# Two-layer recurrent and attention block: the first pair's transposed input rounded by halves of its rows, and the last tile order at the end

## The chip, the cores and the metric

The kernel runs on one NeuronCore of a Trainium2 chip. The metric is the time of one execution on the device, in microseconds (us). The engines are called TensorE (PE in the profile, with its weight loads as PEld), VectorE (DVE), ScalarE (ACT), GpSimd (POOL) and SyncE (SP, which issues the transfers here).

## The reference

The input `x` has shape (4, 512, 256): four batches of 512 tokens. Two layers follow each other, and each has the same outer form:

```
xn = layernorm(x)
s  = attention_or_recurrence(xn)          # layer 0: recurrence, layer 1: causal attention
up_gate = xn @ W1.T ; up_lin = xn @ W3.T  # (tokens, 1024)
hidden  = fwht(silu(up_gate) * up_lin)    # Walsh-Hadamard transform
g  = silu(hidden @ W2.T)
x  = x + s * g
```

The recurrence starts from a zero state and takes one step, so it is a linear map of `xn` followed by an RMS norm, plus `xn`. The change touches the start of layer 0 (its layer norm, the transposition of `xn` and the first products with W1 and W3) and the end of layer 1 (the last products with W2, the Silu, and the final sum).

## The kernel before, in words

**Number format.** Every float32 operand of a product is split into a high part, rounded to the PE's reduced format by a ScalarE copy (CAST in the profile), and a low part, which is the difference taken by VectorE. A product is then three matmuls: high by high, low by high, high by low.

**Tiles.** A batch has four token tiles of 128 tokens. Activations are kept transposed (features on partitions) for the products with W1 and W3. `xT` of batch 0 is the tile `xt` in the profile, with two row halves `k` of 128 features each and 512 token columns. The hidden dimension of 1024 is worked in eight chunks `c` of 128, each with a gate half and a linear half (`f_0gu` in the profile, one bank of the accumulator memory each). Weights W1 and W3 come in four pieces `w13(q)`, q = 0 to 3, each for two chunks.

**The start.** `norm_first` (lines 379 to 428) does batch 0. VectorE takes the statistics of token tiles 0 and 1, then of 2 and 3, and writes `xn` one token tile at a time (line 404). In the meantime TensorE runs eleven products of zeros (`warm`, line 932), then the transposes of the first pair of token tiles, two more zero products, and the transposes of the second pair. A pair's four transposes (two token tiles by two row halves) fill one tile `xt0_0tp` of 128 by 512 float32, which is 2 KiB per partition. ScalarE copies it out as the high part (line 419), and VectorE subtracts for the low part (line 421). The order within each engine is written out by hand with `after(...)`, which puts an instruction behind another in its engine's order.

`split_w13` (line 122) splits a piece of W1 and W3; piece 0 is split in two halves, and the call `next(normed)` between them puts the second half of it behind the transposes.

**The first products.** In `ffn` (line 465) chunk 0 of batch 0 is worked in two halves of the tokens (`parts=2`), so that it can begin with the first pair of token tiles. For each half there are twelve products of 256 columns in three groups of four: high weights by high `xT`, low weights by high `xT`, high weights by low `xT` (line 517). Within a group the gate half takes both row halves `k`, then the linear half. Silu (line 526) and the product with the linear half (line 527) follow each chunk, and VectorE's queue then also holds the preparation of W2 (`w2b`, lines 155 and 156).

**The order elsewhere.** Outside the places with `after`, a scheduler orders each engine's instructions at build time from its own estimate of times. In layer 1 the TensorE order is fixed by hand (`line["fixed"]`).

**The end.** `ffn_s` for the last batch ends with a list of down products (lines 681 to 685): a unit is (q, c, t), three matmuls of 256 columns for token tile `t`. When a tile is complete, `gate_tile` (line 1055) does its Silu on ScalarE (line 1058), the product with `s` and the sum with `x` on VectorE (lines 1059 and 1060), and issues the store from SyncE (line 1061).

Of the kernel before, what the change touches and what calls it, by code (L numbers as in the profile page):

```python
# [35 lines left out]
def kernel(ctx: ExitStack, tc: tile.TileContext, a: dict, out: bass.AP):  # L36
    nc = tc.nc
# [21 lines left out]
    def split(src, hi, lo, engine=nc.vector):  # L59

        h = nc.scalar.copy(hi, src)  # L61
        return h, engine.tensor_tensor(lo, src, hi.bitcast(F32), ALU.subtract)  # L62
# [59 lines left out]
    def split_w13(layer, q, raw):  # L122
        both = wp.tile([P, 2, 2, S], F32R, tag="w13", name=f"w13_{layer}_{q}", bufs=4)
        hi, lo = both[:, 0], both[:, 1]
        if (layer, q) != (0, 0):
            split(raw, hi, lo)
            return hi, lo
        halves = [slice(c * D, (c + 1) * D) for c in range(2)]
        split(*(z[:, :, halves[0]] for z in (raw, hi, lo)))
        next(normed)  # L130
        with after(first["norm"][0]), after(first["norm"][1]):
            hi_, lo_ = split(*(z[:, :, halves[1]] for z in (raw, hi, lo)))
        first["w13"] = hi_, lo_
        return hi, lo
# [85 lines left out]
    def sl(i):  # L220
        return slice(i * P, (i + 1) * P)
# [157 lines left out]
    def norm_first():  # L379

        xn = act.tile([P, NT, D], F32, tag="xn", name="xn0_0", bufs=3)
        hi, lo = xTs[0, 0] = xt_pair("xt0_0")
        xns[0, 0] = xn
        x = xs[0]
        ins, pairs = None, []
        for i in range(2):
            st = act.tile([P, NT, 6], F32, tag="stats", name=f"ln0_0st{i}", bufs=4)
            mv = act.tile([P, NT, 2], F32, tag="mv", name=f"ln0_0mv{i}", bufs=4)
            r = small(f"ln0_0r{i}")
            with after(ins):  # L390
                for t in (2 * i, 2 * i + 1):
                    nc.vector.bn_stats(st[:, t, :], x[:, t, :])
                for t in (2 * i, 2 * i + 1):
                    nc.vector.bn_aggr(mv[:, t, :], st[:, t, :])
                rs = r[:, 2 * i : 2 * i + 2]
                ins = nc.vector.tensor_scalar(
                    rs, mv[:, 2 * i : 2 * i + 2, 1], LN_EPS, None, ALU.add
                )
            nc.gpsimd.tensor_tensor(rs, rs, mhalf[:, :2], ALU.pow)
            pairs.append((mv, r))  # L400
        for i, (mv, r) in enumerate(pairs):
            for t in (2 * i, 2 * i + 1):
                with after(ins):
                    ins = nc.vector.tensor_scalar(
                        xn[:, t, :], x[:, t, :], mv[:, t, 0:1], r[:, t : t + 1], ALU.subtract, ALU.mult
                    )
        yield

        hi_ = lo_ = None
        ins = zero_products(11)  # L410
        for i in range(2):
            ts_ = slice(2 * i * P, 2 * (i + 1) * P)
            o = psum(f"xt0_0tp{i}", [P, 2, 2 * P])
            with after(ins):
                for t in (2 * i, 2 * i + 1):
                    for k in range(2):
                        ins = transpose(o[:, k, sl(t - 2 * i)], xn[:, t, sl(k)], ident)
            with after(hi_):
                hi_ = nc.scalar.copy(hi[:, :, ts_], o)
            with after(lo_):  # L420
                lo_ = nc.vector.tensor_tensor(
                    lo[:, :, ts_], o, hi[:, :, ts_].bitcast(F32), ALU.subtract
                )
            if i == 0:
                with after(ins):
                    ins = zero_products(2)
        first["norm"] = hi_, lo_
        yield
# [33 lines left out]
    def after(ins):  # L462
        return tc.issue_after(ins.ins) if ins else nullcontext()

    def ffn(name, xT, w13, w2, slot, defer=1, spare=(), parts=1, behind=False, tail=()):

        w2h, w2l = w2  # L470
        dn, outs, firsts = [], [], {}

        def down(c, hh, hl, tiles=range(NT)):
            if not dn:
                dn.extend(psum(f"{name}dn{i}", [P, 2, D], tag="dn", bufs=2) for i in range(2))
                outs.extend(dn[t // 2][:, t % 2, :] for t in range(NT))
            for t in tiles:
                o = outs[t]
                for n, (l, r) in enumerate(((hh, w2h), (hh, w2l), (hl, w2h))):
                    first = c == 0 and n == 0  # L480
                    stop = c == NH - 1 and n == 2

                    def one(start):
                        return matmul(
                            o, l[:, sl(t)], r[:, c, :], start=start, stop=stop, skip_group_check=True
                        )

                    if first and t % 2 == 1:  # L490
                        with tc.issue_after(firsts[t // 2].ins):
                            ins = one(False)
                    elif first:
                        ins = firsts[t // 2] = one(True)
                    else:
                        ins = one(False)
            return ins

        queue, gates, late = [], [], []
        for c in range(NH):  # L500
            with after(gates[-2] if behind and c >= 2 else None):
                wh, wl = w13(c // 2)
            gu = []
            for j in range(2):

                o = psum(f"{name}gu{c}_{j}", [P, S], **(DN[0] if behind and c == 1 else GU))
                cols = slice((c % 2) * D + j * P, (c % 2) * D + (j + 1) * P)
                gu.append((o, cols))
            for half in range(parts if c == 0 else 1):
                n = S // (parts if c == 0 else 1)  # L510
                ts_ = slice(half * n, (half + 1) * n)
                if parts == 1 or c:
                    for o, cols in gu:
                        last_up = mm3(o[:, ts_], k_pairs((wh, wl), cols, xT, ts_))
                    continue

                for n, (w, x) in enumerate(((wh, xT[0]), (wl, xT[0]), (wh, xT[1]))):
                    for o, cols in gu:
                        for k in range(2):
                            last_up = matmul(  # L520
                                o[:, ts_], w[:, k, cols], x[:, k, ts_],
                                start=n + k == 0, stop=n + k == 3,
                            )
            gu = [o for o, _ in gu]
            h = hid(f"{name}h{c}")
            first["silu"] = nc.scalar.activation(h, gu[0], AF.Silu)
            gates.append(nc.vector.tensor_tensor(h, h, gu[1], ALU.mult))  # L527
            first["gate"] = gates[-1]
            if c < len(spare):
                hh, hl = spare[c]  # L530
            else:
                hh = hid(f"{name}hh{c}", F32R)
                hl = hid(f"{name}hl{c}", F32R)
            if c < len(spare):
                nc.scalar.copy(hh, h)
                late.append((hl, h, hh))
            else:
                split(h, hh, hl)
            for _ in range(2 if c >= NH - 2 else 0):
                if late:  # L540
                    lo_, h_, hi_ = late.pop(0)
                    with after(gates[-1]):
                        nc.vector.tensor_tensor(lo_, h_, hi_.bitcast(F32), ALU.subtract)
            queue.append((c, hh, hl))
            ups = last_up if behind else None
            with after(gates[-1] if behind else None), after(ups):
                slot(2 * c)
            if len(queue) > defer:
                down(*queue.pop(0))
            with after(gates[-1] if behind else None), after(ups):  # L550
                slot(2 * c + 1)
        line["fixed"] = bool(tail)
        line["last"] = last_up
        for what in tail:
            what()
        for q in queue:
            down(*q)
        return dn

    def ffn_s(name, b, pairs, w2, beside, before, last=None):  # L560
# [119 lines left out]
            return behind, dns  # L680
        for q, c, t in (
            (2, 0, 2), (2, 1, 2), (2, 0, 3), (2, 1, 3), (3, 0, 0), (3, 1, 0), (3, 0, 1), (3, 1, 1),
            (3, 0, 2), (3, 0, 3), (3, 1, 2), (3, 1, 3),
        ):
            down(q, c, hidden[q], (t,))
            if (q, c) == (3, 1):
                last(t, outs[t])
# [258 lines left out]
    first = {"table": None}  # L946
# [245 lines left out]
```

## Time and profile before

| | |
|---|---|
| median of 3 runs | 359.23 us (359.09 to 359.24) |
| the profiled execution's own time | 359.27 us |
| its span, first to last instruction | 357.5 us |
| TensorE busy (matmul, weight load) | 351.5 us, 327.4 us |
| VectorE, ScalarE, GpSimd busy | 287.1, 197.6, 20.8 us |
| mean share of the transfer engines | 41.0% on the main queue |

The span begins with the first instruction and ends with the last; the time of the execution has 1.8 us around it. Rows of the timeline give the start and the length of an instruction, or of several alike in a row (`x4`), in us from the start of the span, and in brackets the idle time of that engine just before and what ended it. Matmuls are pipelined, so a row of one matmul is longer than the step from one to the next. Tiles are named `out<-in`, without their buffer numbers.

### The profile page before, as it was taken

Reading aid. Unit: us, or ns where it says so; the run is one execution under the profiler, and the core shown is the slowest. Engines: PE = TensorE matmul, PEld = TensorE weight load, DVE = VectorE, ACT = ScalarE, POOL = GpSimd, SP = SyncE. Lnnn points to the kernel's source line nnn. Section 1 sums busy time; section 2 is a strip of 40 time slices with the busy share of each in tenths; the row PEclk is TensorE's granted clock in tenths of the full one; section 3 lists DMA queues with packets and bytes.
Section 4 is the critical chain, followed back from the end, with each engine's and each line's share of the span. In section 5 each row is a group of like instructions: output and inputs, shape, how many; then the busy total and the mean of one; then the engine's idle time right before and its main releaser. Section 6 shows DMA issues by size and latency. Waiting matters only on the chain.

```text
span 357.5 us, 6272 instructions
## 1 busy us (share of the span) xinstructions
PE 351.5 (98%) x2477; PEld 327.4 (92%) x2477; DVE 287.1 (80%) x597; ACT 197.6 (55%) x373; POOL 20.8 (6%) x22
## 2 busy tenths in 40 slices
PE   8999999999999999999999999999999999999995
PEld 6878998888988898888999999999999999999995
DVE  6899648998579938898887957989679897568645
ACT  3666156256373424674367655576555676556443
POOL 2000110300020210100110001100011000000000
PEclk9999999999999999999999999999999999999999
DMA  7935000301044416656357145562554745345401
GB/s 222 357 95 202 2 1 2 92 25 61 0 151 160 163 27 219 256 177 198 129 208 254 27 191 207 205 224 105 205 193 150 230 169 205 142 150 192 194 2 59
DMA packets 16284, 52.25 MB, mean 146 GB/s; under 512 B 1632, under 2 KB 7936, under 8 KB 16256
## 3 DMA queue, kind: packets, MB, share of 16 engines
q1 hardware_dynamic: 15968, 51.60, 41.0%
q8 instruction: 19, 0.31, 0.4%
q10 hardware_dynamic: 288, 0.26, 0.2%
q14 instruction: 9, 0.07, 0.1%
HBM read 42.40 MB, written 9.45 MB: 145 GB/s over the span
## 4 chain that ended last, share of the span: by engine, by line
PE 98%; DVE 1%; ACT 0%; issue 0%; DVEq 0%
PE f_1dn L70 6%; PE f_2dn L70 6%; PE f_1gu L70 6%; PE f_0dn L70 6%; PE f_0gu L70 6%; PE f_2gu L70 6%; PE f_3gu L70 6%; PE f_3dn L70 6%; PE sc L70 4%; PE pv L70 4%; PE o L70 3%; PE v L70 3%; PE tq L70 3%; PE warm L70 2%; PE w2ps L70 1%; PE pt L70 1%
## 5 line engine op out<-in xcount | busy, mean ns | idle before, releaser
L70 PE MATMUL f_1gu<-xt,w 128*128 128x512 f32 x96 | 24.9, 396 | 0.3 <-ACT xt L61 0.3
L70 PE MATMUL f_3gu<-xt,w 128*128 128x512 f32 x96 | 25.0, 396 | 0.0
L70 PE MATMUL f_2gu<-xt,w 128*128 128x512 f32 x96 | 24.8, 395 | 0.0
L70 PE MATMUL f_0gu<-xt,w 128*128 128x512 f32 (+1 forms) x108 | 24.4, 379 | 0.0
L70 PEld LDWEIGHTS f_0gu<-xt,w 128*128 128x128 f32 x108 | 18.5, 188 | 4.5 <-issue 1.0
L70 PEld LDWEIGHTS f_1gu<-xt,w 128*128 128x128 f32 x96 | 17.0, 188 | 3.6 <-ACT xt L61 0.5
L70 PEld LDWEIGHTS f_2gu<-xt,w 128*128 128x128 f32 x96 | 17.0, 188 | 3.0
L70 PEld LDWEIGHTS f_3gu<-xt,w 128*128 128x128 f32 x96 | 17.0, 188 | 2.9
L61 ACT CAST f_2hh<-f_2h 128x512 fp32r<-128x512 f32 x16 | 10.0, 622 | 15.3 <-DVE f_2h L527 12.2
L70 PE MATMUL f_3dn<-w2l,f_3hh 128*128 128x256 f32 x64 | 17.7, 281 | 0.0
L70 PE MATMUL f_1dn<-w2l,f_1hh 128*128 128x256 f32 x64 | 17.7, 281 | 0.0
L70 PE MATMUL f_3dn<-w2h,f_3hh 128*128 128x256 f32 x64 | 17.7, 281 | 0.0
L70 PE MATMUL f_2dn<-w2h,f_2hh 128*128 128x256 f32 x64 | 17.7, 282 | 0.0
L70 PE MATMUL f_1dn<-w2h,f_1hh 128*128 128x256 f32 x64 | 17.6, 280 | 0.0
L70 PE MATMUL f_2dn<-w2l,f_2hh 128*128 128x256 f32 x64 | 17.6, 280 | 0.0
L70 PE MATMUL f_3dn<-w2h,f_3hl 128*128 128x256 f32 x64 | 17.0, 281 | 0.0
L70 PE MATMUL f_1dn<-w2h,f_1hl 128*128 128x256 f32 x64 | 17.0, 281 | 0.0
L70 PE MATMUL f_2dn<-w2h,f_2hl 128*128 128x256 f32 x64 | 16.7, 281 | 0.0
L61 ACT CAST f_3hh<-f_3h 128x512 fp32r<-128x512 f32 (+1 forms) x17 | 10.0, 594 | 10.2 <-DVE f_3h L527 6.0
L61 ACT CAST f_1hh<-f_1h 128x512 fp32r<-128x512 f32 x16 | 9.9, 622 | 9.7 <-DVE f_1h L527 6.6
L62 DVE TENSOR_TENSOR f_2hl<-f_2h,f_2hh 128x512 fp32r<-128x512 f32 x16 | 11.0, 686 | 4.5 <-ACT f_2hh L61 4.5
L62 DVE TENSOR_TENSOR f_3hl<-f_3h,f_3hh 128x512 fp32r<-128x512 f32 (+1 forms) x17 | 11.1, 655 | 3.7 <-ACT f_3hh L61 3.6
(487 smaller groups left out, 1149.0 us busy)
## 6 DMA issues: line engine op xcount, KB each, us to landing
sw<-s SPq DMA_DIRECT2D x32, 896.0 KB, 5.3
s<-sp SPq DMA_DIRECT2D x8, 512.0 KB, 4.6
s<-sp SPq DMA_DIRECT2D x8, 384.0 KB, 2.8
w2raw<-in_w SPq DMA_DIRECT2D x4, 512.0 KB, 5.4
sraw<-in_w SPq DMA_DIRECT2D x4, 512.0 KB, 3.3
mrb<-there SPq DMA_DIRECT2D x4, 512.0 KB, 3.7
w13raw<-in_w SPq DMA_DIRECT2D x3, 512.0 KB, 6.8
x<-in_x SPq DMA_DIRECT2D x3, 512.0 KB, 3.6
```

What stands on the lines that cost most here:

```text
L61: h = nc.scalar.copy(hi, src)
L62: return h, engine.tensor_tensor(lo, src, hi.bitcast(F32), ALU.subtract)
L70: ins = call(*args, **kwargs)
```

## The change

There are four edits.

1. In `norm_first` the transposes of a pair run with the row half `k` outside and the token tile inside. For the first pair ScalarE rounds each row half by an instruction of its own, placed after that half's two transposes; for the second pair it rounds the whole as before.
2. In `ffn` the first chunk's products run with `k` outside and gate or linear half inside.
3. In `split_w13` the splits of pieces 2 and 3 are put behind the Silu of chunk 0 and of chunk 1.
4. In the list at the end, unit (3, 1, 2) goes ahead of unit (3, 0, 3).

```diff
     def split_w13(layer, q, raw):
         both = wp.tile([P, 2, 2, S], F32R, tag="w13", name=f"w13_{layer}_{q}", bufs=4)
         hi, lo = both[:, 0], both[:, 1]
-        if (layer, q) != (0, 0):
-            split(raw, hi, lo)
+        if q:
+            with after(first["silus"][q - 2] if q > 1 else None):
+                split(raw, hi, lo)
             return hi, lo
...
             o = psum(f"xt0_0tp{i}", [P, 2, 2 * P])
-            with after(ins):
-                for t in (2 * i, 2 * i + 1):
-                    for k in range(2):
+            for k in range(2):
+                with after(ins):
+                    for t in (2 * i, 2 * i + 1):
                         ins = transpose(o[:, k, sl(t - 2 * i)], xn[:, t, sl(k)], ident)
-            with after(hi_):
-                hi_ = nc.scalar.copy(hi[:, :, ts_], o)
+                if i == 0:
+                    with after(hi_):
+                        hi_ = nc.scalar.copy(hi[:, k, ts_], o[:, k, :])
+            if i:
+                with after(hi_):
+                    hi_ = nc.scalar.copy(hi[:, :, ts_], o)
             with after(lo_):
...
                 for n, (w, x) in enumerate(((wh, xT[0]), (wl, xT[0]), (wh, xT[1]))):
-                    for o, cols in gu:
-                        for k in range(2):
+                    for k in range(2):
+                        for o, cols in gu:
                             last_up = matmul(
...
             first["silu"] = nc.scalar.activation(h, gu[0], AF.Silu)
+            first.setdefault("silus", []).append(first["silu"])
...
             (2, 0, 2), (2, 1, 2), (2, 0, 3), (2, 1, 3), (3, 0, 0), (3, 1, 0), (3, 0, 1), (3, 1, 1),
-            (3, 0, 2), (3, 0, 3), (3, 1, 2), (3, 1, 3),
+            (3, 0, 2), (3, 1, 2), (3, 0, 3), (3, 1, 3),
```

## The prediction

> **What bounds the kernel now.** I read the page's busy times and its chain first, then the waits of TensorE and of its weight loads over the whole span, then the timeline of the two places that the change touches: the first ten microseconds and the last five.
>
> ```profile
> PE 351.5 (98%) x2477; PEld 327.4 (92%) x2477; DVE 287.1 (80%) x597; ACT 197.6 (55%) x373; POOL 20.8 (6%) x22
> ...
> PE 98%; DVE 1%; ACT 0%; issue 0%; DVEq 0%
> ```
>
> ```profile
> PE warm L70 <- DVE zr L929: 1.4, 1, 1.4
> PE f_1gu L70 <- ACT xt L61: 0.3, 1, 0.3
> ```
>
> TensorE is busy 98% of the span, and the chain is TensorE nearly throughout. Its real waits are the start (1.4 us) and one of 0.3 us at 51.6 us, which itself hangs on transposes that TensorE has just made. So a delay of TensorE near the start has nothing behind it that could swallow it: it goes to the end whole. What matters is when the first gate product starts. The timeline of 5 to 10.3 us, with narrow windows for single weight loads:
>
> ```profile
> 6.35 0.53 PEld L70 LDWEIGHTS xt_0tp<-ident,xn 128*128 128x128 f32 x4 [0.56 <-DVE xn L404]
> 6.67 0.15 PEld L70 LDWEIGHTS xt_0tp<-ident,xn 128*128 128x128 f32 x1
> 6.85 0.30 PEld L70 LDWEIGHTS warm<-zr 128*128 128x128 f32 x2
> 7.16 0.59 ACT L419 CAST xt<-xt_0tp 128x512 fp32r<-128x512 f32 x1 [0.56 <-PE xt_0tp L70]
> 7.36 0.53 PEld L70 LDWEIGHTS xt_0tp<-ident,xn 128*128 128x128 f32 x4 [0.20 <-DVE xn L404]
> 7.42 0.70 PE L70 MATMUL xt_0tp<-ident,xn 128*128 128x128 f32 x4
> 7.68 0.14 PEld L70 LDWEIGHTS xt_0tp<-ident,xn 128*128 128x128 f32 x1
> 7.85 2.62 PEld L70 LDWEIGHTS f_0gu<-xt,w 128*128 128x128 f32 x21
> 8.14 1.32 DVE L421 TENSOR_TENSOR xt<-xt_0tp,xt 128x512 fp32r<-128x512 f32 x2
> 8.88 0.19 PEld L70 LDWEIGHTS f_0gu<-xt,w 128*128 128x128 f32 x1
> ```
>
> The reader is to see that the first product's weight load (7.85) follows the second pair's last transpose at the usual step. That pair waits for VectorE's xn (loads at 7.36 and 7.68). ScalarE's rounding of the first pair is over at 7.16 + 0.59 = 7.75, before it is needed. **So what the first part of the change makes shorter is not what the first product waits for.**
>
> **The change part by part.** *1. The first pair by halves of its rows.* Before, four transposes fill one 2 KiB bank, and one ScalarE instruction rounds all of it while TensorE goes on in other banks. After, TensorE makes two transposes (row half k=0 of both token tiles), ScalarE rounds them, and TensorE then writes the k=1 transposes into the same bank. In the built program's order the third transpose now carries a wait for ScalarE, and that is the first of the two half roundings. It had none on ScalarE. Queued behind it on TensorE, in order, are the fourth transpose, two zero products, the second pair's transposes and every product of the kernel.
>
> The trace of before has no case of TensorE writing a bank that ScalarE is reading, so this wait is bounded from both sides. [...] By the row above alone (7.16, TensorE and ScalarE side by side in different banks) it would be nothing. [...]
>
> The working, from two rows: one of the view of the tile `xt_0tp`, for half a bank on ScalarE (minimum, median and longest in ns), and one of the timeline at 51.6 us:
>
> ```profile
> L756 ACT COPY b<-xt_0tp x1: 385/385/385, 145.0 to 145.0; 128x256 f32<-128x256 f32 x1
> ```
>
> ```profile
> 51.60 0.19 PEld L70 LDWEIGHTS f_1gu<-xt,w 128*128 128x128 f32 x1 [0.53 <-ACT xt L61]
> ```
>
> - The second transpose now has to wait for xn tile 1, as the third did: load at 6.67 as before. The four end at 7.12 (6.35 + 0.77 in the timeline), in steps of 0.11, so this one ends at 7.01.
> - ScalarE starts 0.04 after a transpose ends (7.12 to 7.16): 7.05. Half a bank takes 0.385: done at 7.43.
> - From ScalarE's end to TensorE's load: 0.05 (the cast before 51.60 runs from 50.97 for 0.58). The third transpose loads at 7.48 where it stood at 6.67: **+0.81**.
> - Slack behind it: the first transpose of the second pair starts at 7.42, just as the second zero product frees the array (7.19 + 0.23): none. Its third one is loaded at 7.68 for xn and not at about 7.58, as the step of 0.11 would have it: 0.10, which falls away. **-0.10**, so the first gate product comes 0.71 later.
> - Before, the ninth product waits for the low half of xT (load at 8.88, the one before it at 8.67, 0.21 instead of 0.12). After, the second half rounding ends at 7.93 + 0.04 + 0.385 = 8.36 and VectorE's subtraction at about 9.07, while TensorE needs it at 9.57. That stall goes: **-0.08**.
> - Next in line: the second pair's rounding ends near 9.45 and is needed at 9.97; the second half of the first weights is rounded by 9.97 and needed at 10.9; its low part ends near 10.75 and is needed at 12.65. All covered.
>
> *2. Products with k outside.* The same 16 products with the same loads: 0. But the gate bank is now finished by the second to last product, so the first Silu (11.76 before) comes one step, 0.12, later relative to TensorE, and with it the VectorE queue behind it. The tightest user is the low part of the second weights: VectorE ends it at 14.19 + 1.22 = 15.41, and its first load stands at 15.52. The cover is 0.06 after the 0.05 of the semaphore. But a load may come some 0.1 later before the product waits, since 512 columns take 0.23 and a load is followed by its product after 0.12. Between 0 and +0.06; I take **+0.02**.
>
> *3. Weights 2 and 3 not before the Silu of chunk 0 and 1.* In the built order only the rounding of weights 3 moves, ahead of one rounding of a hidden chunk on ScalarE. Their users come microseconds later (weights 3 from 25 us on; ScalarE idles there). Weights 2 wait for their transfer at 13.35, after the later Silu's end (about 13.1). No VectorE, GpSimd or SP instruction and no transfer changes its place. **0**.
>
> *4. The end.* Tile 2's last three products go ahead of tile 3's first group. Tile 2's Silu starts 0.35 earlier (352.56 for 352.92), but VectorE is busy with tile 1 until 353.33, and its order stays: product 2, product 3, sum 2, sum 3. Product 3 waits for tile 3's Silu, which waits for TensorE's last product, and that has not moved.
>
> ```profile
> 352.92 0.74 ACT L1058 ACTIVATE gl<-f_3dn 128x256 f32<-128x256 f32 x2 [0.68 <-PE f_3dn L70]
> ...
> 353.33 0.78 DVE L1059 TENSOR_TENSOR gl<-gl,xn 128x256 f32<-128x256 f32 x2
> ...
> 354.03 0.76 DVE L1060 TENSOR_TENSOR x<-x,gl 128x256 f32<-128x256 f32 x2
> ```
>
> So both sums, and the stores behind them on SP's queue, stand where they stood: **0**, at most -0.1 if the two Silus or two products crowd each other less than I read.
>
> **Sum:** 0.81 - 0.10 - 0.08 + 0.02 = +0.65 us. The profiled execution took 359.27 (span 357.5 and 1.8 around it) and the median is 359.23, so the sum moves over unchanged: 359.9. The lower end of the known costs is about +0.45 (a quicker restart of TensorE, 0.1 at the end). The upper is about +0.9: at 51.60 the restarted products stand 0.34 apart instead of 0.23, 0.1 more, and the tight cover of part 2 and some queue that I called covered may give the rest.
>
> **The rivals.**
> *A. The halves overlap as written: the third transpose doesn't lose by the wait.* It loads by about 6.78, so that the 0.10 of slack still hides it. Then part 1 costs nothing; it also gains nothing, for the first product is held by xn tile 3 and the stall at 8.88 by VectorE's queue (its weight subtraction runs from 7.54 to 8.23). 359.2, not slower. For it: the addresses are disjoint. Against it: the wait in the built order[...]. The point that decides is whether the third load is later than 6.78.
> *B. The clock.* TensorE starts slow: 11 zero products take 5.06 us, 0.43 apart, against 0.23 later. The new idle stretch of about 0.55 us comes just after it has become fast. [...] For it: the stretch falls in the first microsecond at the fast rate. Against it: [...]the idle stretch of 0.33 us at 51.6 slowed nothing after it.
> *C. Faster.* The end gives more than I read (sum 2 before product 3 would bring both stores forward, up to 0.4) and A holds as well: 358.8 to 359.1. The built order speaks against both.
>
> **How the numbers follow.** The main case (+0.65, 359.6 to 360.2) gets 0.86, A 0.06, B 0.05, C 0.03. About what a measurement of this kernel can tell from no change is 0.2%, 0.72 us, and my sum lies just under it. The terms left open (restart, tight cover, later queues) mostly point upward, so I put a little more than half of the main case above the line: 0.47 above, 0.39 below. Slower: 0.47 + 0.05 = 0.52. Within: 0.39 + 0.06 and part of C, 0.46. Faster: 0.02. The range from 359.4 to 360.4 takes in the bounds of the main case and leaves out most of A, B and C.
>
> **What would show it.** In the changed profile: ScalarE's rounding of the first pair as two rows of about 0.38; an idle stretch of about 0.6 on the weight loads, ended by ScalarE, with the third transpose's load near 7.48; the first gate load near 8.56; no gap where 8.88 stood; TensorE's last product about 0.65 later and everything after it unchanged. Wrong if the third transpose loads near 6.7 (A), if products of 256 columns stand 0.2 apart after 8.6 (B), or if the time from TensorE's last product to the end is shorter by more than 0.1 (C).

## The result: a loss of 0.62 us, from a wait before the third transpose

| | before | after |
|---|---|---|
| median of 17 runs each, on one chip | 359.19 us | 359.81 us |
| ratio, 95% interval | | 1.0021 (1.0013 to 1.003) |
| the profiled execution's own time | 359.27 us | 359.67 us |
| its span | 357.5 us | 357.9 us |

The change makes the kernel slower by 0.62 us. The page shows the same bound as before, TensorE, and the line of its chain reads word for word as it did before.

```profile
PE 351.4 (98%) x2477; PEld 327.4 (91%) x2477; DVE 287.0 (80%) x597; ACT 197.8 (55%) x374; POOL 20.8 (6%) x22
```

ScalarE has one instruction more (374), the second half rounding. What is new stands in the waits of TensorE over the whole span of the changed kernel (us in total, times, longest):

```profile
PE warm L70 <- DVE zr L935: 1.5, 1, 1.5
PE xt_0tp L70 <- ACT xt L421: 0.5, 1, 0.5
PE f_1gu L70 <- ACT xt L61: 0.3, 1, 0.3
```

The middle line did not exist before: the transposes (`xt_0tp`) wait once for ScalarE's copy out of their own tile. The timeline of the changed kernel from 5 to 10.9 us shows where:

```profile
5.73 0.73 DVE L405 TENSOR_SCALAR xn<-x,ln_0mv,ln_0r 128x256 f32<-128x256 f32 x2
...
6.51 0.14 PEld L70 LDWEIGHTS xt_0tp<-ident,xn 128*128 128x128 f32 x1 [0.18 <-DVE xn L405]
...
6.88 0.37 ACT L421 CAST xt<-xt_0tp 128x256 fp32r<-128x256 f32 x1 [0.25 <-PE xt_0tp L70]
...
7.31 0.20 PEld L70 LDWEIGHTS xt_0tp<-ident,xn 128*128 128x128 f32 x2 [0.65 <-ACT xt L421]
...
7.79 0.37 ACT L421 CAST xt<-xt_0tp 128x256 fp32r<-128x256 f32 x1 [0.53 <-PE xt_0tp L70]
7.83 0.59 PEld L70 LDWEIGHTS xt_0tp<-ident,xn 128*128 128x128 f32 x4
...
8.39 2.64 PEld L70 LDWEIGHTS f_0gu<-xt,w 128*128 128x128 f32 x22
```

Read it as a relay. The second transpose is loaded at 6.51. ScalarE rounds the first half from 6.88 to 7.25. The third transpose is loaded at 7.31, after the first of the two roundings and not beside it. Everything that TensorE still has to do stands behind it in order: the fourth transpose, two zero products, the second pair's transposes (7.83). So the first gate product is loaded at 8.39.

In this profiled execution VectorE happened to begin `xn` at 5.73 and not at 5.89 as in the trace of before, so the two traces are compared from there.

```profile
5.89 0.73 DVE L404 TENSOR_SCALAR xn<-x,ln_0mv,ln_0r 128x256 f32<-128x256 f32 x2
```

The first gate load comes 8.39 - 5.73 = 2.66 after `xn`, against 7.85 - 5.89 = 1.96 before: +0.70.

The last rows of TensorE, ScalarE and VectorE, from the timeline of the changed kernel from 352.2 us on:

```profile
352.96 0.38 ACT L1064 ACTIVATE gl<-f_3dn 128x256 f32<-128x256 f32 x1 [0.33 <-PE f_3dn L70]
...
353.01 0.75 DVE L1066 TENSOR_TENSOR x<-x,gl 128x256 f32<-128x256 f32 x2
...
353.36 0.28 PE L70 MATMUL f_3dn<-w2h,f_3hl 128*128 128x256 f32 x1
...
353.69 0.83 DVE L1065 TENSOR_TENSOR gl<-gl,xn 128x256 f32<-128x256 f32 x2
354.43 0.75 DVE L1066 TENSOR_TENSOR x<-x,gl 128x256 f32<-128x256 f32 x2
```

Tile 2's Silu (352.96) now runs before TensorE's last product ends, and is over at 353.34. But VectorE takes it up at 353.69 only, when it is nearly through with the sums of tiles 0 and 1 (the row at 353.01, which ends at 353.76). The two sums end at 355.18, which is 1.54 after the last product's end (353.64). Before they ended at 354.79, 1.55 after the end of the last product at 353.24 (its row is below). The end is unchanged to within 0.01.

A useful single number for all kernels below is the time from the first row of `xn` to the start of TensorE's last product, which leaves out when the input landed and what follows at the end. The row of before is (one product, 0.28 long; the product ahead of it starts at 352.84, 0.12 earlier)

```profile
352.96 0.28 PE L70 MATMUL f_3dn<-w2h,f_3hl 128*128 128x256 f32 x1
```

Before the time is 352.96 - 5.89 = 347.07, and after 353.36 - 5.73 = 347.63: +0.56 in these two executions, beside +0.62 in the medians.

### The profile page after: what moved, and what is told of

It reads as the page before. It is cut to its first block, busy times and chain, and to the rows that moved or that the text cites. A ratio compares the mean times of both kernels' runs of the same rounds, so it can differ in the third digit from the quotient of the medians.

```text
span 357.9 us, 6273 instructions
## 1 busy us (share of the span) xinstructions
PE 351.4 (98%) x2477; PEld 327.4 (91%) x2477; DVE 287.0 (80%) x597; ACT 197.8 (55%) x374; POOL 20.8 (6%) x22
## 4 chain that ended last, share of the span: by engine, by line
PE 98%; DVE 1%; ACT 0%; issue 0%; DVEq 0%
PE f_1dn L70 6%; PE f_2dn L70 6%; PE f_1gu L70 6%; PE f_0dn L70 6%; PE f_0gu L70 6%; PE f_2gu L70 6%; PE f_3gu L70 6%; PE f_3dn L70 6%; PE sc L70 4%; PE pv L70 4%; PE o L70 3%; PE v L70 3%; PE tq L70 3%; PE warm L70 1%; PE w2ps L70 1%; PE pt L70 1%
## 5 line engine op out<-in xcount | busy, mean ns | idle before, releaser
L61 ACT CAST f_2hh<-f_2h 128x512 fp32r<-128x512 f32 x16 | 9.9, 622 | 15.6 <-DVE f_2h L533 12.5
L62 DVE TENSOR_TENSOR f_2hl<-f_2h,f_2hh 128x512 fp32r<-128x512 f32 x16 | 10.9, 683 | 4.5 <-ACT f_2hh L61 4.5
```

## The experiments

The theory: the half rounding and the third transpose use one bank of the accumulator memory (a bank is here one buffer of the kernel's `psum` pool, 128 by 512 float32), the wait between them is the whole loss, and the other three edits are worth nothing. The rivals: the loss lies in another edit (the product order, the held weights, the end), or the halving itself costs, with or without the shared bank. Each kernel was timed beside the kernel before, whose medians were 359.22 (E1 to E4) and 359.23 (E5 to E8).

| kernel | median | ratio to before (95%) | first `xn` row to first gate load | to last product |
|---|---|---|---|---|
| before (profile as shown) | 359.19 to 359.23 | 1 | 1.96 | 347.07 |
| changed | 359.81 | 1.0021 (1.0013 to 1.003) | 2.66 | +0.56 |
| E1 all but edit 1 | 359.27 | 1.0002 (0.9994 to 1.0011) | 1.95 | -0.01 |
| E2 edits 1 and 3 | 359.79 | 1.002 (1.0013 to 1.0028) | 2.66 | +0.58 |
| E3 halves in two banks | 359.18 | 0.9998 (0.9989 to 1.0006) | 2.07 | -0.03 |
| E4 both pairs, in line | 360.47 | 1.0035 (1.0022 to 1.0049) | 3.39 | +1.32 |
| E5 both pairs | 359.82 | 1.0016 (1.0009 to 1.0022) | 2.42 | +0.59 |
| E6 no zero products | 359.44 | 1.0009 (1.0 to 1.0018) | 2.29 | +0.34 |
| E7 edit 1 alone | 361.69 | 1.0068 (1.0056 to 1.0081) | 2.65 | +3.05 |
| E8 the end on GpSimd | 360.16 | 1.0026 (1.0016 to 1.0035) | see there | see there |

### E1: all but the rounding

The changed kernel with edit 1 undone:

```diff
-            for k in range(2):
-                with after(ins):
-                    for t in (2 * i, 2 * i + 1):
+            with after(ins):
+                for t in (2 * i, 2 * i + 1):
+                    for k in range(2):
                         ins = transpose(o[:, k, sl(t - 2 * i)], xn[:, t, sl(k)], ident)
-                if i == 0:
-                    with after(hi_):
-                        hi_ = nc.scalar.copy(hi[:, k, ts_], o[:, k, :])
-            if i:
-                with after(hi_):
-                    hi_ = nc.scalar.copy(hi[:, :, ts_], o)
+            with after(hi_):
+                hi_ = nc.scalar.copy(hi[:, :, ts_], o)
```

> The changed kernel with the transposes and the rounding of the first pair as before; the other three edits (products with k outside, weights 2 and 3 behind the Silus, the order at the end) stay. If the bank wait is the whole cost: 359.2, no change from before (within 0.1), the stall ahead of the ninth product back, the first gate load at its old place 0.17 after the last transpose's load. If the k order of the products or the moved weights cost something: 359.5 or more. If the end alone gains: 359.1 or less, with the time from TensorE's last product to the end 0.1 shorter.

Measured 359.27, which can't be told from before. The first gate load is back at 1.95 after `xn`. The product order, the held weights and the end together are worth nothing measurable, so the loss needs edit 1.

### E2: the rounding and the weights alone

The changed kernel with edits 2 and 4 undone:

```diff
-                    for k in range(2):
-                        for o, cols in gu:
+                    for o, cols in gu:
+                        for k in range(2):
...
-            (3, 0, 2), (3, 1, 2), (3, 0, 3), (3, 1, 3),
+            (3, 0, 2), (3, 0, 3), (3, 1, 2), (3, 1, 3),
```

> The kernel before with the rounding by halves and the weights behind the Silus, without the k order of the products and without the new order at the end. If the bank wait is the cost: 359.8 (+0.6), as the changed kernel, with one idle stretch of 0.65 on the weight loads ended by ScalarE. If it takes the k order of the products to make the loss: 359.2.

Measured 359.79: the loss of the changed kernel to 0.02. In the timeline of E2 the third transpose has the same wait:

```profile
7.12 0.20 PEld L70 LDWEIGHTS xt_0tp<-ident,xn 128*128 128x128 f32 x2 [0.66 <-ACT xt L421]
```

Its second transpose is loaded at 6.32, 0.80 earlier. With E1 this places the whole loss in edit 1, with edit 3 beside it (E7 shows what edit 1 does without it).

### E3: the halves in two banks

If the shared bank is the cause, halving costs nothing once each half has a bank of its own. The changed kernel with the first pair's row halves in two banks, and the low part taken in two subtractions:

```diff
-            o = psum(f"xt0_0tp{i}", [P, 2, 2 * P])
+            if i == 0:
+                banks = [psum(f"xt0_0tp0_{k}", [P, 2, 2 * P])[:, 0, :] for k in range(2)]
+            else:
+                o = psum(f"xt0_0tp{i}", [P, 2, 2 * P])
+                banks = [o[:, k, :] for k in range(2)]
...
-                        ins = transpose(o[:, k, sl(t - 2 * i)], xn[:, t, sl(k)], ident)
+                        ins = transpose(banks[k][:, sl(t - 2 * i)], xn[:, t, sl(k)], ident)
...
-                        hi_ = nc.scalar.copy(hi[:, k, ts_], o[:, k, :])
+                        hi_ = nc.scalar.copy(hi[:, k, ts_], banks[k])
...
+            if i == 0:
+                for k in range(2):
+                    with after(lo_):
+                        lo_ = nc.vector.tensor_tensor(
+                            lo[:, k, ts_], banks[k], hi[:, k, ts_].bitcast(F32), ALU.subtract
+                        )
```

> The changed kernel, but the two row halves of the first pair are transposed into two banks, so that the third transpose has nothing to wait for on ScalarE; the low part of the pair is then two subtractions instead of one. If the shared bank is the cause: the idle stretch goes, the third transpose loads 0.06 after the second, and the time is 359.2 to 359.3 (the two subtractions end 0.07 later than one, which the ninth product may wait for). If the two short roundings themselves or the order of the transposes cost the time: 359.8 still. If the halves bring the first product forward, as they look meant to: below 359.1; the theory says no, since the first product is held by the second pair's xn.

Measured 359.18: the loss is gone, with the rounding still in two halves. The timeline of E3 from 5.8 to 10 us:

```profile
6.49 0.31 PEld L70 LDWEIGHTS xt_0tp<-ident,xn 128*128 128x128 f32 x3 [0.19 <-DVE xn L405]
...
6.89 0.64 ACT L425 CAST xt<-xt_0tp 128x256 fp32r<-128x256 f32 x2
...
7.50 0.31 PEld L70 LDWEIGHTS xt_0tp<-ident,xn 128*128 128x128 f32 x3 [0.18 <-DVE xn L405]
```

The second, third and fourth transposes are one unbroken row (`x3` from 6.49 on), while ScalarE's two halves run back to back beside TensorE. This is what the edit seems to have been written to do. It brings nothing: the first gate product still follows the second pair's transposes, which wait for VectorE. It even comes 0.11 later (2.07 after `xn`, 1.96 before): with the row half outside, three of that pair's transposes stand behind its second `xn` tile (7.50, `x3`), where two did. The ninth product's stall is gone here, 0.09, and pays for most of it. Of the kernels run, none was measurably faster than before.

### E4 and E5: the second pair by halves too

A cause that is understood can be doubled. In both kernels the second pair is also rounded by halves in its one bank. In E4 the first product is held behind all transposes, so that nothing can fill the second wait. In E5 it isn't.

```diff
-                if i == 0:
-                    with after(hi_):
-                        hi_ = nc.scalar.copy(hi[:, k, ts_], o[:, k, :])
-            if i:
                 with after(hi_):
-                    hi_ = nc.scalar.copy(hi[:, :, ts_], o)
+                    hi_ = nc.scalar.copy(hi[:, k, ts_], o[:, k, :])
...
+        first["turned"] = ins
...
-                            last_up = matmul(
+                            with after(first["turned"] if half + n + k == 0 else None):
+                                last_up = matmul(
```

(E5 has only the first of the three pieces.)

> The changed kernel with the second pair rounded by row halves too, in one bank, and the first product held behind all eight transposes: the suspected cost twice. If the bank wait is the cost: a second idle stretch of about 0.6 to 0.7, time 360.5 (+1.3 against before). If the cost lies elsewhere (k order, ScalarE's order, clock): 359.8 to 359.9, as the changed kernel. If idle stretches make TensorE lose its clock: 361.5 or more.

E4 measured 360.47, twice the loss of the changed kernel (+1.25). Its timeline has the wait twice:

```profile
7.30 0.20 PEld L70 LDWEIGHTS xt_0tp<-ident,xn 128*128 128x128 f32 x2 [0.72 <-ACT xt L420]
...
8.88 0.20 PEld L70 LDWEIGHTS xt_0tp<-ident,xn 128*128 128x128 f32 x2 [0.70 <-ACT xt L420]
...
9.05 1.13 PEld L70 LDWEIGHTS f_0gu<-xt,w 128*128 128x128 f32 x9
```

The gate loads behind the second wait stand (1.13 - 0.19) / 8 = 0.12 apart, and the granted clock of this execution was 0.997: the two idle stretches cost it no clock that can be seen.

> As the kernel with both pairs rounded by row halves, but the first product is not held behind the transposes: the builder then puts eight products of the first pair between the second pair's two halves. If a bank wait costs only what nothing stands behind to fill: the second wait is covered by 0.94 us of products, one idle stretch instead of two, 359.8 as the changed kernel (+0.6). If the second wait costs by itself, wherever it stands: 360.5, as with the products held.

E5 measured 359.82, the same as the changed kernel with one such wait. Its timeline shows why:

```profile
8.15 1.00 PEld L70 LDWEIGHTS f_0gu<-xt,w 128*128 128x128 f32 x8
...
8.46 0.37 ACT L420 CAST xt<-xt_0tp 128x256 fp32r<-128x256 f32 x1 [0.31 <-PE xt_0tp L70]
9.10 0.24 PEld L70 LDWEIGHTS xt_0tp<-ident,xn 128*128 128x128 f32 x2
```

The builder put eight products between the second pair's halves. ScalarE's rounding (8.46 to 8.83) lies beside them, and the transposes at 9.10 have no bracket: they waited for nothing. The same wait cost 0.7 in E4, where TensorE had nothing else to do (3.39 against 2.66 in the table), and nothing in E5, where it had (359.82 against 359.81).

### E6: without the two zero products

The changed kernel without the two products of zeros between the pairs:

```diff
-            if i == 0:
-                with after(ins):
-                    ins = zero_products(2)
```

> The changed kernel without the two zero products between the pairs. If TensorE's queue, held in order behind the bank wait, is what is late: the zero products now stand on the path, and leaving them out brings 0.46 of the 0.6 back: 359.35 (+0.15). If they are needed to keep the clock fast across the idle stretch: products of 256 columns 0.2 apart after it, 361 or more. If something else holds the first product: 359.8.

Measured 359.44: 0.37 of the loss comes back, a little less than expected. In the timeline of E6 the six transposes left follow each other as soon as ScalarE is done:

```profile
7.29 0.64 PEld L70 LDWEIGHTS xt_0tp<-ident,xn 128*128 128x128 f32 x6 [0.72 <-ACT xt L421]
7.90 2.37 PEld L70 LDWEIGHTS f_0gu<-xt,w 128*128 128x128 f32 x19
```

The first gate load comes 2.29 after `xn`, 0.37 less than in the changed kernel. In this execution ScalarE began its first half 1.26 after `xn` (6.87 - 5.61), and not 1.15 (6.88 - 5.73) as in the changed kernel; that is about what is missing from the 0.46. The products then stand 0.12 apart on the mean, (2.37 - 0.19) / 18, at a granted clock of 1.0, so TensorE kept its clock in this execution without the zero products. No use of them in this place shows here; but leaving them out covers only part of the wait, and the kernel isn't faster than before.

### E7: the rounding alone

Edit 1 alone, on the kernel before, without the order of the weights' splits (edit 3):

```diff
-            with after(ins):
-                for t in (2 * i, 2 * i + 1):
-                    for k in range(2):
+            for k in range(2):
+                with after(ins):
+                    for t in (2 * i, 2 * i + 1):
                         ins = transpose(o[:, k, sl(t - 2 * i)], xn[:, t, sl(k)], ident)
-            with after(hi_):
-                hi_ = nc.scalar.copy(hi[:, :, ts_], o)
+                if i == 0:
+                    with after(hi_):
+                        hi_ = nc.scalar.copy(hi[:, k, ts_], o[:, k, :])
+            if i:
+                with after(hi_):
+                    hi_ = nc.scalar.copy(hi[:, :, ts_], o)
```

> The rounding by halves alone, without the placing of weights 2 and 3, the k order and the end. The builder then puts the rounding of weights 2, whose transfer lands at 13.3, ahead of the first Silu on ScalarE. If that order matters: the first Silu ends at 14.95 instead of 12.9, VectorE's gate product, its W2 steps and the low part of weights 1 behind it come about 2 late, TensorE waits for that low part near 16 to 18 us, 361.5 (+2.3). If there is slack for it: 359.8, as the changed kernel.

Measured 361.69, that is 2.46 more than before and 1.9 more than with edit 3. The two waits of TensorE in E7 on the first products (`f_0gu`), which the changed kernel doesn't have, and then rows of its timeline from 12.5 to 19 us:

```profile
PE f_0gu L70 <- DVE w L62: 1.4, 1, 1.4
PE f_0gu L70 <- ACT f_0h L530: 0.5, 1, 0.5
```

```profile
13.83 1.05 ACT L61 CAST w<-w13raw 128x1024 fp32r<-128x1024 f32 x1 [3.01 <-DMA w13raw<-in_w]
14.79 0.59 ACT L530 ACTIVATE f_0h<-f_0gu 128x512 f32<-128x512 f32 x1
...
17.22 1.22 DVE L62 TENSOR_TENSOR w<-w13raw,w 128x1024 fp32r<-128x1024 f32 x1
```

ScalarE stands still for 3.01 us until a transfer lands, rounds a piece of the weights at 13.83, and only then does the first Silu (14.79; it stood at 11.76 before). The product behind the Silu and the next weights' low part (VectorE, 17.22) are late by as much, and the two waits of TensorE follow, 1.4 and 0.5. They are of the size of the 1.9, but no more can be read from them: this execution took 362.13, 0.44 above the median, and its last product comes 3.05 later and not 2.46. The first gate load is at 2.65 after `xn`, as in the changed kernel, so the bank wait is there too and the rest comes behind it. With the extra rounding instruction the builder ordered ScalarE's queue differently, and edit 3 pins it. So edit 3 gains nothing against before, but edit 1 needs it.

### E8: the end, with the sums of tiles 0 to 2 on GpSimd

The new order of the end did nothing because VectorE is busy with tile 1. Taken off VectorE, the sums should let tile 2's product start earlier. The kernel before with edit 4 and

```diff
-        nc.vector.tensor_tensor(x, x, g, ALU.add)
+        (nc.vector if t == NT - 1 else nc.gpsimd).tensor_tensor(x, x, g, ALU.add)
```

> The kernel before with the new order at the end, and the last sums of token tiles 0 to 2 on GpSimd, so that VectorE's order is product 0 to 3 and sum 3. If VectorE's queue is what keeps the earlier tile 2 from counting: product 2 starts near 352.98 (353.33 before), sum 3 directly after product 3 near 354.15 (354.37 before), 359.0 (-0.2) if GpSimd's sums take under 0.7 each. If GpSimd's sums are slower, the stores, which SyncE issues in order, wait for sum 2: 359.2 to 359.6.

Measured 360.16, +0.93: slower than either case foreseen. TensorE's last product starts at 352.94 (352.96 before), so the loss lies behind it. The rows of VectorE and GpSimd in E8 from 352.26 us on, one instruction each (narrow windows):

```profile
352.26 0.43 DVE L1059 TENSOR_TENSOR gl<-gl,xn 128x256 f32<-128x256 f32 x1
352.28 1.00 POOL L1060 TENSOR_TENSOR x<-x,gl 128x256 f32<-128x256 f32 x1 [77.54 <-DVE gl L1059]
...
352.97 0.59 DVE L1059 TENSOR_TENSOR gl<-gl,xn 128x256 f32<-128x256 f32 x1 [0.28 <-ACT gl L1058]
...
353.24 0.90 POOL L1060 TENSOR_TENSOR x<-x,gl 128x256 f32<-128x256 f32 x1
...
353.68 0.75 DVE L1059 TENSOR_TENSOR gl<-gl,xn 128x256 f32<-128x256 f32 x1
...
354.10 0.90 POOL L1060 TENSOR_TENSOR x<-x,gl 128x256 f32<-128x256 f32 x1
...
354.46 0.83 DVE L1060 TENSOR_TENSOR x<-x,gl 128x256 f32<-128x256 f32 x1
```

The first half of the idea holds: tile 2's product starts at 352.97 and not at 353.33. Then it turns over. Each sum on GpSimd takes 0.90 to 1.00, and VectorE's own instructions beside them take 0.59, 0.75 and 0.83 where they took 0.42. The last sum ends at 355.29 (354.79 before), and the last store is issued at 355.74 (354.90 before), which is most of the 0.93. Of these 0.84, the later last sum is 0.50. The rest lies in SyncE's queue: it issues tile 3's store when that sum is done (355.31), and tile 2's store, whose own sum was over at 355.00, stands behind it. That edit 4 could gain with VectorE's own queue in another order was not tried.

## Why the prediction was right

**The third transpose, +0.81: right.** Its load stands 0.80 behind the second one's (7.31 - 6.51). The parts: 0.37 from that load to ScalarE's start, 0.37 for half a bank (0.385 was assumed, from a copy in layer 0), 0.06 back to TensorE (7.25 to 7.31). That the third transpose waits at all, though the two halves don't overlap, was read from the built order; that the wait lasts the whole rounding was the author's assumption, since no row of before shows such a case. It did: ScalarE's half ends at 7.25, and the load follows at 7.31. E3 agrees that the shared bank goes with it: the same halves in two banks carry no wait (one unbroken row, 6.49, `x3`) and no loss (359.18). But in E3 each half also has a tile of its own, so whether the builder sets this wait by the bank or by the tile is not shown. Nor is it shown what the chip does when the wait is simply left out; that was not tried.

**The slack, -0.10: right.** The second pair's four loads are one unbroken row (7.83, `x4`). Xn tile 3 no longer holds the third of them. Hence +0.70 at the first gate load, where the steps gave 0.71.

**The ninth product, -0.08: right.** Of the first unbroken gate rows, before has 21 loads in 2.62, that is (2.62 - 0.19) / 20 = 0.121 from one to the next. After has 22 in 2.64, (2.64 - 0.19) / 21 = 0.117. Over 20 steps that is 2.43 and 2.33, a difference of 0.10: the stall that is gone.

**Product order, +0.02: 0.** The later Silu made nothing late; the low part of the second weights still comes in time. E1 and E2 bound the whole of edits 2 to 4 near zero.

**The weights' order, 0: right, for a reason that was missing.** The prediction looked at what edit 3 moves in the finished order and found cover for all of it. It did not ask what the builder would do with edit 1 alone, which is 1.9 us (E7).

**The end, 0: right.** The last sum ends 1.54 after TensorE's last product, 1.55 before.

**The sum.** With the measured terms it is 0.80 - 0.10 - 0.10 + 0 = +0.60, beside +0.62 in the medians. So the number is right by its parts and not by errors that cancel. On which side of its line of 0.72 us the loss would fall, the prediction left nearly open (a little more than half for above); it fell below. That line was too wide for these runs, though: the interval of 1.0013 to 1.003 tells the 0.62 from no change.

**The rivals.** A (no wait) falls: the third load is at 7.31, not near 6.7. B (the clock) falls in this trace: the weight loads idle for 0.65 us and the array for 0.46, yet the gate loads behind stand 0.117 apart, at a granted clock of 0.999. Whether it falls in every execution is open. Among 78 executions of the kernels with this wait (the changed one, E2, E4 to E7), three took about 2 us more than their kernel's median, with a granted clock of 0.994 or 0.995: 361.97 (changed), 361.76 (E2) and 361.36 (E6). Of the 128 without it, none is over 0.6 above its median. The lower clock would fit B, but no trace of the three was kept, and the number is too small to call the cause shown. C (faster) falls with the end.

## What to carry to other kernels

Splitting a copy out of the accumulator memory so that it overlaps its own producer worked here with a bank and a tile for each piece (E3, no wait); within one of them the producer stopped for the copy, 0.80 us from the second load to the third. On TensorE, which is 98% busy here, such a stop cost 0.7 where nothing else could run in it (E4) and nothing where eight products could (E5). And before making something early, look at which wait the consumer really ends on: even with two banks (E3) the early half was worth nothing, because the first product was held by the other pair.

## What the runs showed of the hardware that was not expected

**GpSimd and VectorE take turns in E8.** The slow VectorE instructions aren't slow by a factor. GpSimd's three sums end at 353.28, 354.14 and 355.00. VectorE's three instructions, which start while one of those is running (352.97, 353.68, 354.46), end at 353.56, 354.43 and 355.29. Each ends 0.28 to 0.29 after the GpSimd sum that it met, however long it had then been started. It holds the other way too: each GpSimd sum ends 0.57 to 0.59 after the VectorE instruction that was running when it started (ends at 352.69, 353.56, 354.43). So in these rows it looks as if each is held until the other is done and then does its work. If so, the 0.90 to 1.00 of a sum on GpSimd contain a wait for VectorE. What a sum takes alone, and what holds the two engines apart, no run here shows. The expectation for E8 had not taken it into account.

**One extra instruction can reorder a queue.** In E7 a single additional ScalarE instruction of 0.37 us led the builder to put a copy that waits for a transfer ahead of the first Silu, and the kernel took 1.9 us more. This is a matter of the builder's estimates and not of the chip, but it shows in the trace as if the chip had become slower.
